# Feed-forward products by Strassen's algorithm over pairs of sequences, with features on the partitions

## The chip, the cores and the metric

The kernel runs on one NeuronCore of a Trainium2 chip. The metric is the device time of one execution in microseconds, the median of several runs. The engines are named as the profile names them: PE is TensorE (matrix products, with PEld its weight loads), DVE is VectorE, ACT is ScalarE, POOL is GpSimd, SP is SyncE, which here only issues DMAs.

## The reference

Four sequences of 512 tokens with 256 features pass through a gated scan and then through a feed-forward stack, each with a norm before and behind and a residual around it. All is float32.

```python
x = x + ln(attn(ln(x)))          # ln over the 256 features, no weights
x = x + ln(ffn(ln(x)))

def attn(x):                     # E = 256, HD = 128, E2 = 512
    q = silu(x @ Wq1 @ Wq2);  v = x @ Wv
    a = exp(log_sigmoid(sigmoid(x @ Wk1 @ Wk2)));  k = 1 - a
    h[t] = a[t] * h[t-1] + k[t] * v[t]           # scan over the tokens
    out = q * h
    return (out * rsqrt(mean(out**2) + 1e-6) * norm_w) @ Wo

def ffn(x):                      # 6 blocks, hidden 1024
    for i in range(6):
        x = gelu(x @ W1[i].T + B1[i]) @ W2[i].T + B2[i] + x
        if i < 5: x = ln(x) * LN_G[i] + LN_B[i]
    return x
```

## The kernel before

One sequence is one group of 512 tokens. The norms and the residuals have tokens on the partitions (four tiles of 128 tokens by 256 features); the projections, the gates, the scan and the hidden layer have features on the partitions, so that the scan runs along the free dimension. `transposed` (L122 to L126) turns a normalized group with eight TensorE transposes into two banks of PSUM and copies them out, one on DVE and one on ACT.

The first part is the attention. All loads are issued at the start: x, the constants and the first two blocks of feed-forward weights on SP's queue, the attention's weights on ACT's. The biases and norm weights of the feed-forward part are loaded with one copy for each partition. `won` (L156) is Wo scaled by norm_w. `scan_part` makes, for each of four feature tiles, the products psk, psv and psq, the sigmoids on ACT, and nkv, q and the scan h on DVE; POOL makes o = q h. `out_part` multiplies o by won with tokens on the partitions (psy) and sums the squares with one-column matmuls (pss). It runs one sequence behind the scan.

The second part is the feed-forward stack: six blocks, and in each the four sequences one after another. `hidden_part` (L306, L313) makes eight 128x512 tiles of the hidden layer, two matmuls each, and ACT's Gelu takes each out of PSUM with the bias. `output_part` (L324) uses the hidden tiles as the stationary operand: for each of four token tiles eight 128x256 matmuls into po, then DVE adds the residual (L331) and takes the norm's statistics (L99, L100). The norm's square root is on ACT (L105), with a table load before and behind it, as Gelu has another table. Two DVE instructions normalize and apply the norm's weights (L338, L341), and POOL adds the second bias to what will be the next residual (`with_bias`, L279). The transposes of the next sequence stand between hidden and output part of this one. `ffn_input` joins the parts: it adds the attention's normalized output to x and normalizes again.

Two sets of weights are held (w1 and w2 with two buffers); block i + 1 is loaded when block i begins. The framework's scheduler orders the instructions of each engine and sets the semaphores.

Of the kernel before, what the change touches and what calls it, by code (L numbers as in the profile page):

```python
# [9 lines left out]
F32 = mybir.dt.float32  # L10
AF = mybir.ActivationFunctionType
ALU = mybir.AluOpType
PSUM = bass.MemoryType.PSUM

P = 128
# [3 lines left out]

@with_exitstack  # L20
def kernel(
    ctx: ExitStack,
    tc: tile.TileContext,
    x: bass.AP,  # [B, S, E]
    wq1: bass.AP,  # [E, HD]
    wq2: bass.AP,  # [HD, E2]
    wk1: bass.AP,  # [E, HD]
    wk2: bass.AP,  # [HD, E2]
    wv: bass.AP,  # [E, E2]
    wo: bass.AP,  # [E2, E]  # L30
    norm_w: bass.AP,  # [128, E2/128], column c holds features c*128 ..
    w1t: bass.AP,  # [NB, E, HID]
    b1: bass.AP,  # [128, NB, HID/128], likewise
    w2t: bass.AP,  # [NB, HID, E]
    b2: bass.AP,  # [NB, E]
    ln_g: bass.AP,  # [NB-1, E]
    ln_b: bass.AP,  # [NB-1, E]
    out: bass.AP,  # [B, S, E]
):
    """x += LN(attn(LN(x))); x += LN(ffn(LN(x))), one sequence (512 tokens) as a group.  # L40

    Norms and residuals have tokens on the partitions; projections, the gates and the
    scan have features on the partitions, so that the scan runs along the free dimension.
    """
# [4 lines left out]
    NT = S // P  # token tiles of a group  # L49
# [3 lines left out]
    assert HD == P and S == 512  # L53
# [3 lines left out]
    ypool = ctx.enter_context(tc.tile_pool(name="ypool", bufs=B))  # L57
    small = ctx.enter_context(tc.tile_pool(name="small", bufs=4))
    xtp = ctx.enter_context(tc.tile_pool(name="xtp", bufs=3))
    wpool = ctx.enter_context(tc.tile_pool(name="wpool", bufs=2))  # L60
    ps_t = ctx.enter_context(tc.tile_pool(name="ps_t", bufs=2, space=PSUM))

# [7 lines left out]
    # x of each sequence, token c*128+p at [p, c]; it becomes x + LN(attn) in place.  # L70
    xs = []
    for b in range(B):
        xb = xpool.tile([P, NT, E], F32, tag="x", name=f"x_{b}")
        nc.sync.dma_start(out=xb, in_=x[b].rearrange("(c p) e -> p c e", p=P))
        xs.append(xb)

    b1_s = const.tile([P, NB, NH], F32)
    b2_s = const.tile([P, NB, E], F32)
    g_s = const.tile([P, NB - 1, E], F32)
    be_s = const.tile([P, NB - 1, E], F32)  # L80

    def load_ffn_constants():
        nc.sync.dma_start(out=b1_s, in_=b1)
        for t, src in ((b2_s, b2), (g_s, ln_g), (be_s, ln_b)):
            nc.sync.dma_start(out=t, in_=src.partition_broadcast(P))
# [9 lines left out]

    def token_stats(mv, src, t):
        """mean and variance over the free dim of src [128, E] into mv[:, t, :]"""
        st = small.tile([P, 6], F32, tag="bnst", name="st")
        nc.vector.bn_stats(st, src)  # L99
        nc.vector.bn_aggr(mv[:, t, :], st)  # L100

    def rstd_of(mv):
        """1 / sqrt(var + LN_EPS) of the tiles of a group"""
        std = small.tile([P, NT], F32, tag="std", name="std")
        nc.scalar.activation(std, mv[:, :, 1], AF.Sqrt, bias=eps_t)  # L105
        rstd = small.tile([P, NT], F32, tag="rstd", name="rstd")
        nc.vector.reciprocal(rstd, std)
        return rstd

    def normalized(dst, src, mv, scale, t):  # L110
        """dst = (src - mean) * scale of token tile t"""
        nc.vector.tensor_scalar(  # L112
            dst, src, mv[:, t, 0:1], scale[:, t : t + 1], ALU.subtract, ALU.mult
        )

    def transposed(src):
        """[128 tokens, NT, E] -> [128 features, ND, S]"""
        xt = xtp.tile([P, ND, S], F32, tag="xt", name="xt")
        for d in range(ND):
            pt = ps_t.tile([P, S], F32, tag="pt", name="pt")  # L120
            for t in range(NT):
                nc.tensor.transpose(pt[:, ts(t, P)], src[:, t, ts(d, P)], ident)  # L122
            if d % 2:
                nc.scalar.copy(xt[:, d, :], pt)
            else:
                nc.vector.tensor_copy(xt[:, d, :], pt)  # L126
        return xt

    ys, yscale_in, ymv = [None] * B, [None] * B, [None] * B

    with ExitStack() as actx:
# [3 lines left out]
        xnp = actx.enter_context(tc.tile_pool(name="xnp", bufs=B))  # L135
        ps_m = actx.enter_context(tc.tile_pool(name="ps_m", bufs=4, space=PSUM))
        ps_y = actx.enter_context(tc.tile_pool(name="ps_y", bufs=1, space=PSUM))

# [4 lines left out]
        wq2_s = aw.tile([P, E2], F32)  # L143
        nc.scalar.dma_start(out=wq2_s, in_=wq2)
# [3 lines left out]
        nc.scalar.dma_start(out=wv_s, in_=wv.rearrange("(c p) f -> p c f", p=P))  # L148
        wo_s = aw.tile([P, NE, E], F32)
        nc.scalar.dma_start(out=wo_s, in_=wo.rearrange("(c p) e -> p c e", p=P))  # L150
        nw_s = aw.tile([P, NE], F32)
        nc.scalar.dma_start(out=nw_s, in_=norm_w)
        # norm_w scales the rows of Wo: (out * norm_w) @ Wo
        won = aw.tile([P, NE, E], F32)
        for e in range(NE):
            nc.vector.tensor_scalar(  # L156
                won[:, e, :], wo_s[:, e, :], nw_s[:, e : e + 1], None, ALU.mult
            )

        load_ffn_constants()  # L160
        load_weights(0)
        load_weights(1)
        xns = []
        for b in range(B):
            mv = small.tile([P, NT, 2], F32, tag="mv", name="mv")
            for t in range(NT):
                token_stats(mv, xs[b][:, t, :], t)
            rstd = rstd_of(mv)
            xn = xnp.tile([P, NT, E], F32, tag="xn", name="xn")
            for t in range(NT):  # L170
                normalized(xn[:, t, :], xs[b][:, t, :], mv, rstd, t)
            xns.append(xn)

        def hidden(w1_s, xt, name):
            ps = ps_m.tile([P, S], F32, tag="m", name=f"ps_{name}")
            for d in range(ND):
                nc.tensor.matmul(  # L177
                    ps, w1_s[:, d, :], xt[:, d, :], start=(d == 0), stop=(d == ND - 1)
# [5 lines left out]
        def scan_part(b, xt):  # L184
            q1 = hidden(wq1_s, xt, "q1")
            k1 = hidden(wk1_s, xt, "k1")
            o = opool.tile([P, NE, S], F32, tag="o", name="o")
            sq = opool.tile([P, NE, S], F32, tag="sq", name="sq")
            for e in range(NE):
                psk = ps_m.tile([P, S], F32, tag="m", name="psk")  # L190
                nc.tensor.matmul(psk, wk2_s[:, ts(e, P)], k1, start=True, stop=True)  # L191
                psv = ps_m.tile([P, S], F32, tag="m", name="psv")
                for d in range(ND):
# [3 lines left out]
                        xt[:, d, :],  # L197
                        start=(d == 0),
                        stop=(d == ND - 1),
                    )  # L200
                psq = ps_m.tile([P, S], F32, tag="m", name="psq")
                nc.tensor.matmul(psq, wq2_s[:, ts(e, P)], q1, start=True, stop=True)  # L202

                # exp(log_sigmoid(f)) is sigmoid(f)
# [7 lines left out]
                # nkv = (a - 1) v;  h_t = a_t h_(t-1) - nkv_t  # L212
# [8 lines left out]
            return o, sq  # L221

        def out_part(b, o, sq):
            """y = (out * norm_w) @ Wo before the RMS scale r, with its mean and variance.

            LN(r y) = (y - mean) / sqrt(var + LN_EPS / r^2), 1/r^2 = mean(out^2) + RMS_EPS.
            """
            y = ypool.tile([P, NT, E], F32, tag="y", name=f"y_{b}")
            mv = ypool.tile([P, NT, 2], F32, tag="ymv", name=f"ymv_{b}")
            pss = ps_y.tile([P, NT], F32, tag="ss", name="pss")  # L230
            for t in range(NT):
                psy = ps_y.tile([P, E], F32, tag="y", name="psy")
# [177 lines left out]
```

## Time and profile before

| | us |
|---|---|
| runs | 860.53, 856.35, 859.64; median 859.64 |
| span of the profiled execution | 853.8 |
| PE busy | 815.0 (95%) |
| DVE, ACT, POOL busy | 310.7, 278.7, 109.4 |
| first feed-forward product in the chain of waits | 161.47 |
| 32 ph instructions of one sequence | 13.73 to 13.79 |
| 64 po instructions of one sequence | 13.81 |
| mean granted TensorE clock | 0.983 |

The span runs from the first to the last instruction of one execution; the page gives no other time of that execution, so the device time of the runs is set beside it. Busy time is the time in which an engine has an instruction running; for PE the end of a matmul is modelled. In a row of a group the two numbers behind the bar are the total busy time and the mean duration of one, and then comes the idle time of the engine before these instructions, with what ended it. One float32 matmul of the code appears as two MATMUL instructions in the trace.

### The profile page before, as it was taken

The numbers are of one execution on the slowest core, as the hardware profiler recorded it, in microseconds if no ns is written. First come the engines' busy times: TensorE is split into PE (matmuls) and PEld (weight loads), VectorE is DVE, ScalarE is ACT, GpSimd is POOL, SyncE is SP. The second block draws the span as 40 slices with busy tenths as digits, with TensorE's granted clock in tenths as the row PEclk, the third lists the DMA queues.
The fourth block names the chain that finished last, engine by engine and source line by source line (L and its number), as shares of the span: only waits on it lengthen the run. The fifth ranks groups of instructions, "written<-read, shape, count | busy, mean of one in ns | idle before, by whom it ended". The sixth has DMA issues, their size and how long they took to land.

```text
span 853.8 us, 7481 instructions
## 1 busy us (share of the span) xinstructions
PE 815.0 (95%) x2944; PEld 536.8 (63%) x2944; DVE 310.7 (36%) x750; ACT 278.7 (33%) x403; POOL 109.4 (13%) x134
## 2 busy tenths in 40 slices
PE   1999998699999999999999999999999999999996
PEld 0447657376577567765776577657765776577655
DVE  4562551725542334233423342334233423331223
ACT  1463451424421422242224222422243224322430
POOL 0120210201040111011101110111011101110111
PEclk9998999799999999999999999999999999999998
DMA  9400000000001100011000020000110000000000
GB/s 333 147 1 0 1 1 0 1 0 1 0 1 50 49 1 0 1 50 49 1 1 0 1 99 1 1 0 1 50 49 1 0 1 1 0 25 0 26 25 25
DMA packets 14674, 21.21 MB, mean 25 GB/s; under 512 B 944, under 2 KB 12208, under 8 KB 14640
## 3 DMA queue, kind: packets, MB, share of 16 engines
q1 hardware_dynamic: 12864, 18.90, 6.4%
q10 hardware_dynamic: 1776, 1.84, 0.6%
q8 instruction: 23, 0.38, 0.2%
q14 instruction: 11, 0.09, 0.0%
HBM read 18.64 MB, written 2.10 MB: 24 GB/s over the span
## 4 chain that ended last, share of the span: by engine, by line
PE 92%; issue 3%; DVE 2%; DMA 2%; POOL 0%; ACT 0%; POOLq 0%; ACTq 0%; DVEq 0%
PE ph L306 38%; PE po L324 37%; PE psy L234 4%; PE psv L194 3%; PE pt L122 3%; PE pss L242 2%; PE psk L191 2%; PE psq L202 2%; DMA nw_s<-in_norm_w 1%; PE ps_q L177 1%; PE ps_k L177 1%; DMA wk_s<-in_wk 1%; DVE xn L112 0%; DVE st L99 0%; DVE z L112 0%
## 5 line engine op out<-in xcount | busy, mean ns | idle before, releaser
L306 PE MATMUL ph<-xt,w 128*128 128x512 f32 x768 | 336.6, 596 | 0.9 <-DVE xt L126 0.9
L324 PE MATMUL po<-w,ht 128*128 128x256 f32 x1536 | 335.5, 379 | 0.0
L324 PEld LDWEIGHTS po<-w,ht 128*128 128x128 f32 x1536 | 290.0, 190 | 38.9 <-issue 0.5
L306 PEld LDWEIGHTS ph<-xt,w 128*128 128x128 f32 x768 | 146.4, 191 | 176.3 <-issue 170.7
L313 ACT ACTIVATE ht<-ph,b_s 128x512 f32<-128x512 f32 x192 | 129.4, 687 | 141.2 <-PE ph L306 140.9
L279 POOL TENSOR_TENSOR res<-f,b_s 128x256 f32<-128x256 f32 x96 | 76.7, 821 | 533.5 <-DVE f L341 438.3
L331 DVE TENSOR_TENSOR s<-po,res 128x256 f32<-128x256 f32 x96 | 40.8, 425 | 243.7 <-PE po L324 230.4
L105 ACT ACTIVATE std<-mv,eps_t 128x4 f32<-128x4 f32 x32 | 9.5, 297 | 282.2 <-DVE mv L100 282.0
L126 DVE COPY xt<-pt 128x512 f32<-128x512 f32 x28 | 19.3, 690 | 184.4 <-PE pt L122 184.4
L338 DVE SCALAR_TENSOR_TENSOR z<-s,mv,g_s 128x256 f32<-128x256 f32 x80 | 53.7, 691 | 1.4
L105 ACT ACT_TABLE_LOAD x29 | 37.2, 1283 | 51.9 <-DVE mv L100 44.0
L99 DVE BATCH_NORM_STATS2 st<-s 128x6 f32<-128x256 f32 x96 | 41.1, 428 | 3.3
L234 PE MATMUL psy<-won,o 128*128 128x256 f32 x128 | 35.5, 426 | 2.4 <-ACT y L249 2.4
L122 PEld LDWEIGHTS pt<-ident,f 128*128 128x128 f32 x192 | 22.9, 143 | 20.3 <-issue 18.8
L341 DVE SCALAR_TENSOR_TENSOR f<-z,rstd,be_s 128x256 f32<-128x256 f32 x80 | 35.5, 484 | 0.6
L234 PEld LDWEIGHTS psy<-won,o 128*128 128x128 f32 x128 | 26.7, 213 | 13.3 <-ACT y L249 5.5
L313 ACT ACT_TABLE_LOAD x27 | 34.6, 1283 | 0.5
L219 POOL TENSOR_TENSOR o<-q,h 128x512 f32<-128x512 f32 x16 | 20.3, 1268 | 107.8 <-DVE h L218 57.7
L122 PE MATMUL pt<-ident,f 128*128 128x128 f32 x192 | 26.6, 280 | 6.4 <-DVE f L112 6.4
L194 PE MATMUL psv<-xt,wv_s 128*128 128x512 f32 x64 | 30.1, 592 | 0.0
L347 POOL TENSOR_TENSOR s<-s,x 128x256 f32<-128x256 f32 x16 | 11.8, 764 | 99.8 <-issue 50.1
L122 PE MATMUL pt<-ident,xn 128*128 128x128 f32 x32 | 6.1, 334 | 18.8 <-DVE xn L112 18.1
(48 smaller groups left out, 323.8 us busy)
## 6 DMA issues: line engine op xcount, KB each, us to landing
w<-in_w1t SPq DMA_DIRECT2D x6, 1024.0 KB, 5.1
w<-in_w2t SPq DMA_DIRECT2D x6, 1024.0 KB, 5.6
x<-in_x SPq DMA_DIRECT2D x4, 512.0 KB, 7.6
out<-s SPq DMA_DIRECT2D x16, 128.0 KB, 1.7
b_s<-in_b SPq DMA_DIRECT2D x1, 768.0 KB, 7.7
g_s<-in_ln_g SPq DMA_DIRECT2D x1, 640.0 KB, 8.6
be_s<-in_ln_b SPq DMA_DIRECT2D x1, 640.0 KB, 8.1
wv_s<-in_wv ACTq DMA_DIRECT2D x1, 512.0 KB, 8.4
```

The source lines that it names most:

```text
L99: nc.vector.bn_stats(st, src)
L105: nc.scalar.activation(std, mv[:, :, 1], AF.Sqrt, bias=eps_t)
L122: nc.tensor.transpose(pt[:, ts(t, P)], src[:, t, ts(d, P)], ident)
L194: nc.tensor.matmul(psv, wv_s[:, d, ts(e, P)], xt[:, d, :], start=(d == 0), stop=(d == ND - 1),)
L234: nc.tensor.matmul(psy, o[:, e, ts(t, P)], won[:, e, :], start=(e == 0), stop=(e == NE - 1),)
L279: nc.gpsimd.tensor_tensor(r[:, t, :], f[:, t, :], b2_s[:, i, :], ALU.add)
L306: nc.tensor.matmul(ph, w1_s[:, d, ts(c, P)], xt[:, d, :], start=(d == 0), stop=(d == ND - 1),)
L313: nc.scalar.activation(ht[:, c, :], ph, AF.Gelu, bias=b1_s[:, i, c : c + 1])
L324: nc.tensor.matmul(po, ht[:, c, ts(t, P)], w2_s[:, c, :], start=(c == 0), stop=(c == NH - 1),)
L331: nc.vector.tensor_tensor(s[:, t, :], po, r[:, t, :], ALU.add)
L338: nc.vector.scalar_tensor_tensor(z, s[:, t, :], mv[:, t, 0:1], g_s[:, i, :], ALU.subtract, ALU.mult)
L341: nc.vector.scalar_tensor_tensor(f[:, t, :], z, rstd[:, t : t + 1], be_s[:, i, :], ALU.mult, ALU.add)
```

## The change

The feed-forward part is rewritten; the attention is reordered with it.

- Two sequences form one group. For each of the two weight products the weights, the features and the two sequences are seen as 2 by 2 blocks, and seven block products (Winograd's form of Strassen's algorithm) stand for eight. A hidden tile pair takes seven 128x512 matmuls instead of eight, the output part 28 instead of 32.
- The weights' block sums s1 to s4 are made on POOL, eight 128x512 additions for each block. The input's block sums t1 to t4 are made on DVE and POOL, for the normalized input (`tx`) and for each hidden tile pair (`tc`).
- Products p1, p6, p7 and p4 add up in one bank (px); after each ACT copies the running sum out (`sn`), or in the output part DVE adds it to the residual and the bias. The others are added to these copies by DVE before the Gelu.
- Both products have the weights as the stationary operand, so the output has features on the partitions. `norm_part` transposes it to tokens, takes the statistics, normalizes on DVE, and transposes back; the norm's weight and bias are applied when the second transposes are copied out. The constants are now one column for each feature tile.
- TensorE's order is written by hand (`manual_schedule`, `interleaved`): the norm of one pair of sequences stands in pieces between the products of the other pair, one piece after each fifth product.
- In the attention x of the first sequence is loaded in four pieces, some loads move from ACT's queue to SP's, k comes before q, won is made on POOL, POOL adds pairs of squares so that pss has half the matmuls, and out_part and the first `ffn_input` are interleaved with the scan of later sequences.

```diff
+    ctx.enter_context(tc.manual_schedule(engines={PE}))
...
+    def block_sums(a11, a12, a21, a22, shape, tag):
...
+        tt = nc.gpsimd.tensor_tensor
+        tt(s1, a21, a22, ALU.add)
+        tt(s3, a11, a21, ALU.subtract)
+        tt(s2, s1, a11, ALU.subtract)
+        tt(s4, a12, s2, ALU.subtract)
...
+    def to_features(src, d, tag, pool, scale=None, bias=None):
...
+        elif d % 2:
+            nc.scalar.activation(xt, pt, AF.Identity, scale=scale, bias=bias)
+        else:
+            nc.vector.tensor_scalar(xt, pt, scale, bias, ALU.mult, ALU.add)
...
+                if e % 2:
+                    nc.gpsimd.tensor_tensor(
+                        sq[:, e, :], sq[:, e, :], sq[:, e - 1, :], ALU.add
+                    )
...
+    def token_sums(b11, b12, b21, b22, pool, tag, engines):
...
+        engines[0].tensor_tensor(t1, b12, b11, ALU.subtract)
+        engines[2].tensor_tensor(t3, b22, b12, ALU.subtract)
+        engines[1].tensor_tensor(t2, b22, t1, ALU.subtract)
+        engines[3].tensor_tensor(t4, b21, t2, ALU.subtract)
...
+            def copied(self):
+                s = snp.tile([P, S], F32, tag="sn", name="sn")
+                nc.scalar.copy(s, self.px)
+                return s
...
+            def added(self, half, n, ps, s):
+                nc.vector.tensor_tensor(self.new(half, n), ps, s, ALU.add)
+                self.gelu(half, n)
...
+                engines = (POOL, DVE, POOL, DVE) if j < NP - 1 else (DVE, DVE, POOL, DVE)
+                tc4[j] = token_sums(*ht[j], *ht[NP + j], tcp, "tc", engines)
+
+        for j in range(0, NP, 2):
+            a, c = Pair(j), Pair(j + 1)
+            yield from a.p1()
+            yield from a.p2()
+            yield from c.p1()
+            yield from a.p6()
+            yield from c.p2()
+            yield from c.p6()
+            yield from a.p7()
+            yield from a.p5()
+            yield from c.p7()
+            yield from a.p4()
+            yield from c.p5()
+            yield from c.p4()
+            yield from a.p3()
+            yield from c.p3()
...
+        yield from product(px, a11, b11, True)
+        sn1 = partial(px, x11, 0)
+        yield from product(py, a12, b21, True)
+        nc.vector.tensor_tensor(sf[0][0], py, sn1, ALU.add)
+        yield from product(px, s2, t2, False)
+        sn2 = partial(px, x12, 0)
+        yield from product(pz, s1, t1, True)
+        yield from product(px, s3, t3, False)
+        sn3 = partial(px, x22, 1)
+        nc.vector.tensor_tensor(sf[1][1], pz, sn3, ALU.add)
+        yield from product(px, a22, t4, False)
+        with_bias(sf[1][0], px, x21, 1)
+        yield from product(pz, s4, b22, False)
+        nc.vector.tensor_tensor(sf[0][1], pz, sn2, ALU.add)
...
+    def norm_part(i, g):
...
+                    nc.tensor.transpose(
+                        pt[:, ts(2 * k + d, P)], sf[d][n][:, ts(t, P)], ident
+                    )
...
+            nc.scalar.copy(sm.rearrange("p a b -> p (a b)"), pt)
...
+        rstd = rstd_of(mv, nt)
...
+        for g in range(NG):
+            interleaved(chain_of(hidden_part(i, g), output_part(i, g)), pending, 6, 5)
+            pending = norm_part(i, g)
...
+        if i + 1 < NB:
+            sums1[i + 1] = w1_sums(i + 1)
+            sums2[i + 1] = w2_sums(i + 1)
```

## The prediction

> **What bounds the kernel now.** I read the page first (busy shares, the chain that ended last, the costliest groups), then the chain in order of time, then windows for the clock, then the timeline of single instructions.
>
> ```profile
> span 853.8 us, 7481 instructions
> PE 815.0 (95%) x2944; PEld 536.8 (63%) x2944; DVE 310.7 (36%) x750; ACT 278.7 (33%) x403; POOL 109.4 (13%) x134
> L306 PE MATMUL ph<-xt,w 128*128 128x512 f32 x768 | 336.6, 596 | 0.9 <-DVE xt L126 0.9
> L324 PE MATMUL po<-w,ht 128*128 128x256 f32 x1536 | 335.5, 379 | 0.0
> L313 ACT ACTIVATE ht<-ph,b_s 128x512 f32<-128x512 f32 x192 | 129.4, 687 | 141.2 <-PE ph L306 140.9
> ```
>
> TensorE never waits in the feed-forward part. The chain in order of time gives its pace:
>
> ```profile
> 147.11 2.01 PE psy L234 x8
> 149.56 2.01 PE psy L234 x8
> 157.16 2.19 DVE f L112 x4
> 161.47 9.67 PE ph L306 x16
> ...
> 249.76 13.79 PE ph L306 x32
> 264.42 13.81 PE po L324 x64
> 278.23 13.79 PE ph L306 x32
> ```
>
> A pass over one sequence is 32 ph instructions in 13.73 to 13.79 us, 0.87 us of eight transposes, 64 po in 13.81: 28.42 us. The chip runs each 128x512 product of the code as two instructions, so one product is 13.73 / 16 = 0.858 us. Two sequences take 56.8 us, the whole part 161.5 to 845.9, the tail to the end of the span 7.9.
>
> **TensorE's share of the change.** A pair of sequences is now 56 products (28 hidden, 28 output) instead of 64: 56 x 0.858 = 48.0 us. Features on the partitions cost transposes both ways, 32 instead of 16: 32 x 0.109 = 3.5. That is 51.5 us against 56.8, and 12 x 5.3 = 64 us would be the gain if TensorE still never waited.
>
> **Waits that the products now have.** In Strassen's form one bank, px, holds a running sum: a product is added, the bank is copied out, the next product is added. So TensorE waits for ACT's copies in the hidden part and for DVE's partial sums in the output part, and all engines work in the order of the built program. I laid one steady pair of sequences out by hand against that order with these rows: copy 0.59 (L124, 586), gelu 0.69 (L313), PSUM add 0.68 (q<-psq,sg, 677), SBUF two-input 512 columns on DVE 0.68 (x<-x,z, 417 for 256, most of it per column), the same on POOL 1.27 (o<-q,h, 1268), stats 0.43 and 0.18, matmul end to ACT's start 0.2.
>
> - First half of the hidden part (blocks 0 and 1): two products lie between a copy and its next use, 1.72 us, and 7 copies and gelus per 6 us of products fit on ACT. No wait.
> - Second half: in DVE's order the token sums of blocks 0 and 1 (t2, t4, t2, t4) and two stats stand before the add that makes this half's first gelu input, and in ACT's order that gelu stands before the copy that releases product c.p7. The chain from the end of the first half: gelu ready +0.8, POOL t1 1.27, POOL t3 1.27 and t1 1.27 of the next block, DVE t2 0.68, stats 0.43, t4 0.68, aggregate 0.18, stats 0.43, add 0.69, gelu 0.69, copy 0.59: 9.0 us. TensorE gets there after 8 products and 8 transposes, 7.7. Wait **1.3 us**, if DVE and POOL don't disturb each other.
> - Hidden to output: ACT's order puts the norm's square root with its two table loads before this half's last four gelus, DVE's order the reciprocal and eight normalizations before the last two adds, and the first partial sum of px behind the last token sums. From 0.7 before the hidden part's end: load 1.28, root 0.30, reciprocal 0.18, eight normalizations 2.67 (xn, x8), add 0.69, gelu 0.69, POOL t1 1.27, four DVE sums 2.72, partial 0.69, some 0.4 of hand-overs: ends 10.2 after the hidden part. The first two output products are 8 matmuls and 8 transposes, 7.7. Wait **2.5 us** before the third.
> - Third-last to second-last output product: both add into px with nothing between; drain 0.2, partial 0.69, 0.05: **0.95 us**.
>
> That is 4.75 us of waits at least. The upper end comes from this pair of rows: the same instruction alone, and beside a POOL addition.
>
> ```profile
> 244.10 0.48 DVE L338 SCALAR_TENSOR_TENSOR z<-s,mv,g_s 128x256 f32<-128x256 f32 x1
> ...
> 253.51 0.83 POOL L279 TENSOR_TENSOR res<-f,b_s 128x256 f32<-128x256 f32 x1 [11.47 <-DVE f L341]
> 253.68 0.95 DVE L338 SCALAR_TENSOR_TENSOR z<-s,mv,g_s 128x256 f32<-128x256 f32 x1
> ```
>
> z had 0.66 us of res ahead of it and took 0.47 longer. The token sums are of this kind: DVE's t2 needs POOL's t1, and POOL starts t3 at once, just as t2 becomes ready. If each waits the other's instruction out, the second half's chain gains 2.0 (wait 3.3), the hand-over to the output gains two POOL instructions less an overlap, 2.4 (wait 4.9), and the sums for the next hidden part, which DVE's order puts before the third partial sum, add 1.5 (wait 2.5): 10.7 us. A pair of sequences is then 56.3 to 62.2 us. I take 0.47 / 0.66 = 0.7 of the way, **60.4 us**, against 56.8 before.
>
> [...]
>
> **Before and around the feed-forward part.** First ph was at 161.5.
> - Start: DVE's won waits for norm_w until 16.30, and xn stands behind it at 17.58; won goes to POOL, norm_w and the broadcast constants (2 MB) out of the way. Stats on the first sequence stood at 6.95, but in DVE's new order two stats of the second, whose load was there at 7.33, precede the reciprocal: 8.2; root hidden, reciprocal 0.2, four normalizations 1.35, transposes and copies 2 to 3: first projection near 12 instead of 23.96. -12.
> - The 9.9 us from psy's end at 151.57 to ph: the first input's norm now lies beside the last scan. In its place the last out_part waits for the scan: f 0.60, a 0.63, nkv 0.69, q 0.68, h 1.28, o 1.27, less the three psy and four transposes before it, then the square 0.63 and POOL's new addition 1.27: 5. Net -5.
> - pss is halved: four bursts of 3.46 become 1.7 each, -7; the half clock that follows three of them (0.50 in the windows 68 to 74, 102 to 104, 136 to 138) cost 6, of which I expect 4 back.
> - POOL makes the first block's weight sums (8 x 1.27) before the first o: up to 3 later. +2.5.
> First product at 161.5 - 12 - 5 - 7 - 4 + 2.5 = 136.
> - First pair only: DVE does two sequences of ffn_input inside it, about 2 x 4 x (0.45 + 0.42 + 0.43 + 0.18 + 0.41) = 15 us, and ACT three pairs of table loads; roughly 9 not hidden (4 to 14).
> - Tail: 16 transposes with copies 3, last stats 1, load and root 1.6, norms, eight POOL additions at 0.76, output 2: 15 instead of 7.9.
> - Weight sums of later blocks: eight POOL additions, 10 us per two pairs; POOL has slack, their clash with DVE is in the upper end. Weight loads, 2 MB per block, lie under 100 us of work. Nothing.
>
> **Sum.** 136 + 12 x 60.4 + 9 + 15 = 885 against the profiled span of 853.8. The median of the runs, 859.64, stands 5.8 above that span; the page has no other time of the profiled execution. 885 + 5.8 = **891 us**. Without any DVE-POOL clash 136 + 675 + 24 + 5.8 = 841; with full exclusion 912. Equal times need a pair in (853.8 - 136 - 24) / 12 = 57.8 us, 6.3 us of waits.
>
> **Rivals.**
> 1. *Faster: the clash is small at 512 columns.* DVE's and POOL's instructions slip past each other, waits stay at 4.75 us: 841 us. It decides from under 6.3 us of waits per pair. For it: in the row 254.31 POOL's next res, 0.90, is hardly longer than 0.83. Against it: every z beside a res is near 0.95. 0.29.
> 2. *Much slower: the wait before the third output product drops the clock.* These windows (PE busy, PEld, DVE, ACT, POOL, then the granted clock) show 4.3 us of idle TensorE followed by 0.5:
>
> ```profile
> 152.00:154.00 2.00, 0.00 (x0) 0.00 (x0) 2.00 (x9) 1.27 (x1) 0.00 (x0) 1.00 0.01 4
> 154.00:156.00 2.00, 0.00 (x0) 0.00 (x0) 2.00 (x9) 0.00 (x0) 0.00 (x0) 1.00 0.00 0
> 156.00:158.00 2.00, 0.34 (x2) 0.30 (x2) 1.64 (x8) 0.39 (x2) 0.26 (x1) 0.59 0.00 0
> 158.00:160.00 2.00, 1.65 (x7) 0.96 (x7) 2.00 (x3) 0.00 (x0) 2.00 (x4) 0.50 0.00 0
> ```
>
> A wait of 4.9 is as long; some 3.4 us at half speed (about what the windows from 100.9 to 104.5 show) lose 1.7 in each of twelve pairs: 912 + 20 = 932. Against it: the gaps of 0.4 us at 138 to 152 left the clock at 1.0, and 0.7 of the way means 4.2 us. 0.13.
> 3. *The change doesn't give seven for eight in time.* Products that each wait for their own copy lose the overlap of weight load and drain, as psk<-k does at 49.74: 1.12 us for one product where the one in mid-stream at 41.75 shows 1.02, after 0.30 of waiting. A quarter of a microsecond on some 20 products of a pair is 5 us, 60 in all, on top of rival 1: 901. For it: most hidden products come after a copy or an add that releases their bank. Against it: psq and psk in mid-stream run at the full pace. 0.06.
>
> The forecast itself has 0.52, with 866 to 912 of its own. Under 840 lies perhaps 0.1 (rival 1 with a better start), over 930 as much (rival 2): range **840 to 930**. A difference within 0.5%, 4.3 us, is about what a measurement of this kernel can't tell from no change; rival 1 gives faster 0.25 and same 0.04, the forecast's lower edge 0.04 and 0.02, all else is slower: 0.29, 0.06, 0.65.
>
> **What would show it.** In the changed profile: PE busy near 740 us of a longer span; products at 0.43 per instruction; TensorE waiting three times per pair of sequences, for ACT's sn and DVE's partial sums, 6 to 10 us together; DVE sums of 512 columns above 0.9 us mean where POOL's run; first hidden product near 136 us. I am wrong if these waits are below 6 us per pair, if the sums show 0.7, or if the first product comes far from 136.

## The result and the profile after

The changed kernel takes **930.9 us** (median of four runs, 930.3 to 933.5) against 860.0 (856.4 to 860.5): 1.087 times the time before, 95% interval 1.082 to 1.093. Forecast were 891 us and a range of 840 to 930: the side is right, the size 40 us too low, and the range misses the time by 0.9 us. The profiled execution took 930.8 us, its span is 928.9.

The page after, in the same parts as before: span, busy times, the share of each engine in the chain that ended last, the granted clock in 40 slices, and the groups that matter (total and mean duration, then idle time before them and what ended it).

```profile
span 928.9 us, 6362 instructions
PE 783.4 (84%) x2112; PEld 371.1 (40%) x2112; DVE 522.3 (56%) x930; ACT 352.3 (38%) x565; POOL 251.7 (27%) x194
PEclk9998897999989999899999899998999998999998
PE 36%; DVE 28%; issue 17%; ACT 12%; POOL 5%; DMA 1%; POOLq 0%; DVEq 0%; ACTq 0%
L408 PE MATMUL px<-tc,sb 128*128 128x512 f32 x192 | 110.3, 717 | 41.2 <-DVE sn L530 38.7
L408 PE MATMUL px<-tx,sa 128*128 128x512 f32 x192 | 98.6, 606 | 32.6 <-ACT sn L437 32.6
L394 DVE TENSOR_TENSOR tc<-ht,tc 128x512 f32<-128x512 f32 x48 | 70.9, 1476 | 25.7 <-POOL tc L392 25.7
```

PE is busy 31.6 us less than before and the span is 75.1 longer: TensorE now waits. DVE carries 28% of the last chain. The third output product (px<-tc,sb) shows 717 ns an instruction where undisturbed products show 593: part of it ran at a lower clock (0.50 in the windows below). The row of tc has sums of 512 columns at 1.48 us, twice what the prediction's rows gave for one alone.

What TensorE waited for (us in total, times, longest), from the view of waits:

```profile
PE px L408 <- DVE sn L530: 62.5, 24, 4.2
PE px L408 <- ACT sn L437: 34.6, 15, 2.6
PE pt L163 <- DVE xn L154: 16.0, 3, 12.7
PE pt L163 <- DVE z L154: 7.4, 3, 3.5
```

The first two lines are the feed-forward part, 24 waits for DVE's partial sums and 15 for ACT's copies: nearly all of them stand in the three places that the prediction named. In TensorE's timeline of one steady pair of sequences (start, us, then in brackets the idle time before and its releaser) they are:

```profile
437.08 1.13 PE L408 MATMUL px<-tx,sa 128*128 128x512 f32 x2 [2.61 <-ACT sn L437]
454.01 5.12 PE L408 MATMUL px<-tc,sb 128*128 128x512 f32 x8 [3.53 <-DVE sn L530]
469.09 3.70 PE L408 MATMUL px<-tc,w 128*128 128x512 f32 x8 [2.21 <-DVE sn L530]
```

The eight instructions at 454.01 take 5.12 us, those at 469.09 3.70. The windows around 454 (PE busy, PEld, DVE, ACT, POOL, then the granted clock) say why: 3.5 us of idle TensorE, then half the clock.

```profile
450.00:452.00 2.00, 0.48 (x5) 0.24 (x3) 2.00 (x2) 0.78 (x1) 1.55 (x1) 1.00 0.00 0
452.00:454.00 2.00, 0.00 (x0) 0.00 (x0) 2.00 (x5) 0.00 (x0) 0.00 (x0) 0.88 0.00 0
454.00:456.00 2.00, 1.99 (x3) 0.96 (x4) 1.16 (x2) 0.00 (x0) 0.00 (x0) 0.50 0.00 0
456.00:458.00 2.00, 2.00 (x5) 0.88 (x4) 0.00 (x0) 0.00 (x0) 0.00 (x0) 0.77 0.00 0
```

What DVE did in the meantime, from its timeline:

```profile
443.03 0.20 DVE L149 RECIPROCAL rstd<-std 128x8 f32<-128x8 f32 x1 [2.07 <-ACT std L147]
443.27 2.67 DVE L154 TENSOR_SCALAR n<-sm,mv,rstd 128x256 f32<-128x256 f32 x8
445.86 1.28 DVE L453 TENSOR_TENSOR ht<-pz,sn 128x512 f32<-128x512 f32 x2
...
448.68 1.74 DVE L394 TENSOR_TENSOR tc<-ht,tc 128x512 f32<-128x512 f32 x1 [0.82 <-POOL tc L392]
450.35 1.75 DVE L392 TENSOR_TENSOR tc<-ht 128x512 f32<-128x512 f32 x1
452.02 0.68 DVE L395 TENSOR_TENSOR tc<-ht,tc 128x512 f32<-128x512 f32 x1
```

and POOL, from its own:

```profile
447.37 1.27 POOL L392 TENSOR_TENSOR tc<-ht 128x512 f32<-128x512 f32 x1 [14.10 <-ACT ht L443]
448.60 2.95 POOL L393 TENSOR_TENSOR tc<-ht 128x512 f32<-128x512 f32 x2
```

Two things are seen. The eight normalizations of the other pair of sequences stand in DVE's queue, with 2.07 us of waiting for the square root, ahead of the last two adds of the hidden part (445.86), on which all that follows depends. And a DVE sum that starts just after a POOL sum takes 1.74 or 1.75 us; as soon as POOL is done (451.55) the next takes 0.68. The alternation is a strict one: POOL's two take 2.95 instead of 2 x 1.27.

The first feed-forward product stands at 160.31, hardly earlier than before (161.47).

### The profile page after: what moved, and what is told of

Read it like the earlier page. It is cut to its first block, busy times and chain, and to the rows that moved or that the text cites. A ratio compares the mean times of both kernels' runs of the same rounds, so it can differ in the third digit from the quotient of the medians.

```text
span 928.9 us, 6362 instructions
## 1 busy us (share of the span) xinstructions
PE 783.4 (84%) x2112; PEld 371.1 (40%) x2112; DVE 522.3 (56%) x930; ACT 352.3 (38%) x565; POOL 251.7 (27%) x194
## 3 DMA queue, kind: packets, MB, share of 16 engines
q10 hardware_dynamic: 1104, 1.31, 0.4%
## 4 chain that ended last, share of the span: by engine, by line
PE 36%; DVE 28%; issue 17%; ACT 12%; POOL 5%; DMA 1%; POOLq 0%; DVEq 0%; ACTq 0%
PE px L408 16%; PE pz L408 8%; DVE tc L394 7%; ACT ht L443 5%; DVE n L154 4%; DVE tc L395 3%; POOL tc L392 3%; PE psy L336 3%; DVE ht L453 2%; DVE tc L392 2%; DVE st L141 2%; PE pt L163 2%; ACT L147 2%; PE psv L278 2%; ACT sn L437 1%
## 5 line engine op out<-in xcount | busy, mean ns | idle before, releaser
L443 ACT ACTIVATE ht<-ht,b_s 128x512 f32<-128x512 f32 x144 | 102.6, 721 | 124.9 <-DVE ht L453 77.1
L408 PE MATMUL px<-tc,sb 128*128 128x512 f32 x192 | 110.3, 717 | 41.2 <-DVE sn L530 38.7
L437 ACT COPY sn<-px 128x512 f32<-128x512 f32 x144 | 81.0, 581 | 146.8 <-PE px L408 146.8
L392 POOL TENSOR_TENSOR tc<-ht 128x512 f32<-128x512 f32 x36 | 51.4, 1426 | 314.3 <-ACT ht L443 314.3
L408 PE MATMUL px<-tx,sa 128*128 128x512 f32 x192 | 98.6, 606 | 32.6 <-ACT sn L437 32.6
L394 DVE TENSOR_TENSOR tc<-ht,tc 128x512 f32<-128x512 f32 x48 | 70.9, 1476 | 25.7 <-POOL tc L392 25.7
L453 DVE TENSOR_TENSOR ht<-pz,sn 128x512 f32<-128x512 f32 x96 | 64.6, 684 | 30.3 <-ACT ht L443 17.0
L393 POOL TENSOR_TENSOR tc<-ht 128x512 f32<-128x512 f32 x48 | 71.0, 1490 | 0.0
L530 DVE SCALAR_TENSOR_TENSOR sn<-px,b_s,xt 128x512 f32<-128x512 f32 x36 | 26.7, 742 | 62.0 <-PE px L408 62.0
L408 PE MATMUL px<-tx,w 128*128 128x512 f32 x96 | 52.0, 624 | 2.0 <-ACT sn L437 2.0
L408 PE MATMUL pz<-tx,sa 128*128 128x512 f32 x96 | 49.9, 602 | 0.0
L408 PE MATMUL px<-xt,w 128*128 128x512 f32 x96 | 49.1, 593 | 0.0
```

The lines of the kernel that those rows point to most:

```text
L392: engines[0].tensor_tensor(t1, b12, b11, ALU.subtract)
L393: engines[2].tensor_tensor(t3, b22, b12, ALU.subtract)
L394: engines[1].tensor_tensor(t2, b22, t1, ALU.subtract)
L408: nc.tensor.matmul(ps, l, r, start=start and k == 0, stop=True, skip_group_check=True)
L437: nc.scalar.copy(s, self.px)
L443: nc.scalar.activation(h, h if src is None else src, AF.Gelu, bias=b1_s[:, i, c : c + 1])
```

## The experiments

Theories: **A**, POOL's and DVE's sums exclude each other, and that makes TensorE wait. **B**, the norm's place in DVE's queue, ahead of the last adds and the sums, makes it wait. **C**, the idle time costs a second time, by the clock. For the first product: TensorE's hand-written order in the attention waits for norms. A time in the table is that of one execution, for the changed kernel, e5_all, e6_old_ffn and e7_split the median of four; the kernel before took 852.0 to 859.8 beside them. Where an edit moves work on the other engines, the scheduler orders their queues anew.

| run | edit to the changed kernel | us | PE waits for sn (DVE, ACT) |
|---|---|---|---|
| changed kernel | | 930.9 | 62.5, 34.6 |
| e1_tc_dve | hidden sums all on DVE | 888.7 | 24.3, 11.0 |
| e2_warm | three dummy products before the long wait | 909.4 | 36.1, 33.9 |
| e3_norm_later | norm pieces later | 869.3 | 17.2, 35.8 |
| e4_attn | order of the norms in the attention | 906.1 | 56.4, 34.5 |
| e9_both | e1 and e3 | 820.7 | 10.1, 4.3 |
| e11_no_table | no square root, so no table loads | 950.5 | 70.3, 34.0 |
| e5_all | e1, e3, e4, input sums on DVE, output order | 787.3 | 0, 6.7 |
| e7_split | e5 with the sums shared again | 837.5 | 7.0, 35.8 |
| e8_pool_all | e5 with the hidden sums all on POOL | 810.1 | 0, 6.7 (and 15.3 for tc) |
| e6_old_ffn | e4 with the feed-forward part of before | 825.8 | |

### A alone: the sums of the hidden block on DVE (e1_tc_dve)

```diff
-                engines = (POOL, DVE, POOL, DVE) if j < NP - 1 else (DVE, DVE, POOL, DVE)
+                engines = (DVE, DVE, DVE, DVE)
```

> All four token sums of each hidden tile pair (tc) on DVE; POOL keeps only the weight sums, tx t3 and the attention's work. Theory A (DVE and POOL shut each other out for whole instructions): the sums t2 of 1.48 us mean fall to 0.68, the chain between the halves of the hidden part shortens by about 2 us although DVE now has seven more instructions per pair, and the wait before c.p7 (2.6 us) falls under 1; the wait before the third output product stays near 3.5, since DVE now does eight sums one after another there. About 2 to 3 us per pair of sequences: 895 to 905 us. Theory B (only the place in the queues counts, not the other engine): the sums stay as long in the way, 920 to 935 us.

888.7 us, 42 less. DVE has more instructions and is faster through them. Its groups and TensorE's waits:

```profile
L392 DVE TENSOR_TENSOR tc<-ht 128x512 f32<-128x512 f32 x48 | 35.9, 748 | 0.9 <-ACT ht L443 0.2
L394 DVE TENSOR_TENSOR tc<-ht,tc 128x512 f32<-128x512 f32 x48 | 32.8, 682 | 0.0
```

```profile
PE pz L408 <- DVE ht L453: 24.8, 11, 3.1
PE px L408 <- DVE sn L530: 24.3, 12, 2.3
```

L394 falls from 1476 to 682 ns. The wait before the third output product is gone, where I had expected it to stay near 3.5. A new one takes part of its place (pz for ht, 24.8, 1.30 and 3.07 us in turn): it ends with an add of the hidden part that stands behind six normalizations of the other pair in DVE's queue (in one pair they run from 482.25 to 486.04, the add from 485.96). That is B's place in the queue, still there. A holds, and the gain is larger than I expected of it. It isn't the length of the sums alone: DVE's waiting for POOL's sums (25.7 us in the row of tc of the changed kernel) goes with it.

### C alone: the same wait, with TensorE kept busy (e2_warm)

```diff
         nc.vector.tensor_tensor(sf[0][0], py, sn1, ALU.add)
+        pw = ps_m.tile([P, S], F32, tag="m", name="pw")
+        for k in range(3):
+            nc.tensor.matmul(pw, a12[k], b21[k], start=True, stop=True)
```

> Three extra products into an unused PSUM bank behind the second output product, where TensorE waits 3.5 us; nothing reads them. If the half clock after that wait comes from the idle TensorE, it goes and with it 1.5 us in each of eleven pairs, though TensorE does 31 us more work: 910 to 916 us. If the clock follows something else, or the extra products push the third one back: 930 to 935 us.

909.4 us. The dummy products, which nobody reads, fill 2.6 us of the wait; what is left of it is 0.96 to 1.63, together as long as before, and the product behind takes 3.70 instead of 5.1 to 6.8. The other two waits of a pair stay at 2.55 and 2.21. Ten steady pairs take 614.7 us here and 634.4 in the changed kernel: the half clock costs 2.0 us a pair, some 20 of the 21.5 us. Most of the rest lies ahead of the feed-forward part, which starts about 1.2 us earlier.

### B alone: the norm's pieces later (e3_norm_later)

The first piece of the norm comes after the fourth product instead of the sixth, the next ones after every eighth instead of every fifth. The square root then lies behind the last gelu, and the normalizations behind the sums.

```diff
-            interleaved(chain_of(hidden_part(i, g), output_part(i, g)), pending, 6, 5)
+            interleaved(chain_of(hidden_part(i, g), output_part(i, g)), pending, 4, 8)
```

> The pieces of the other pair's norm stand behind every eighth product from the fourth on, not every fifth from the sixth; in the built order the square root with its table loads then comes behind this half's last gelu and the eight normalizations behind the token sums. Theory B (place in the queues): the wait before the third output product falls from 3.5 us plus 1.5 us of half clock to under 1, that before c.p7 from 2.6 to about 1 as adds now stand before two of the token sums, that before the second-last output product to about 1: 5 to 6 us in each of eleven pairs, 865 to 875 us. Theory A alone (the exclusion of DVE and POOL, wherever they stand): the sums keep their 1.48 us and less than 15 us is won, 915 or more.

869.3 us, 62 less, with the exclusion untouched (L394 at 1480 ns). DVE's timeline at the same point of a pair:

```profile
422.06 0.69 DVE L453 TENSOR_TENSOR ht<-pz,sn 128x512 f32<-128x512 f32 x1 [0.17 <-PE pz L408]
...
424.03 1.74 DVE L394 TENSOR_TENSOR tc<-ht,tc 128x512 f32<-128x512 f32 x1 [0.45 <-POOL tc L392]
...
430.25 2.67 DVE L154 TENSOR_SCALAR n<-sm,mv,rstd 128x256 f32<-128x256 f32 x8
```

The last add runs as its product ends, the sums follow, and the 2.67 us of normalizations lie behind them. The waits for DVE's sn go from 62.5 to 17.2 and no longer drop the clock (the longest is 0.97, and the product behind it takes 3.70). B is the largest single factor. The waits for ACT's sn come to 35.8 as before (34.6), but they are 38 now instead of 15: in place of the 2.6 before one product of the second half of the hidden part a pair has 0.40, 0.63 and 1.73 before three.

### Do A and B cure the same wait? (e9_both)

Both edits, nothing else.

> The changed kernel with two edits that were each tried alone: the hidden block's sums all on DVE (alone: 888.7 us, 42 less than the changed kernel) and the norms behind these sums (alone: 869.3 us, 62 less). If they cure different waits their gains add: 931 - 42 - 62 = 827 us. If they cure the same wait twice over, only the larger one counts: 855 to 869 us. The attention and the order of the output products are untouched, so it should lie above the run with all edits (787) by what those two bring, 25 us for the attention and the rest for the order.

820.7 us: 110 less, where the single gains add to 104. By the expectation the edits then cure different waits, but the waits don't say so. Each edit alone takes away most of the wait before the third output product and the half clock behind it (3.53 to 4.20 us of waiting become 0 in e1 and at most 0.97 in e3). What each leaves behind alone makes up for that: e1 leaves the 24.8 us for ht, behind the norm that e3 moves, and 2.27 before the second-last product, mostly with half clock behind it (the product takes 5.40 us instead of 3.70); e3 leaves the 35.8 for ACT's sn. With both edits the first is gone, the second is 0.84 and the third 4.3. That the gains add is thus a sum that happens to come out. With these two edits the kernel is already some 35 us faster than before (856.1 beside it).

### Is it ACT's table loads? (e11_no_table)

```diff
-        nc.scalar.activation(std, mv[:, :, 1], AF.Sqrt, bias=eps_t)
+        nc.scalar.activation(std, mv[:, :, 1], AF.Sqrt if nt == NT else AF.Identity, bias=eps_t)
```

> The changed kernel, but the square root of the norms behind the output products is left out (ACT copies the variance plus epsilon in its place), so the two table loads of 1.28 us around it go and its place in ACT's queue stays. If the eight normalising instructions ahead of the last hidden sums in DVE's queue are what makes TensorE wait, they still stand there and start 1.3 us earlier: the waits before the third output product fall by 1.3 to 2.6 us of a pair and the half clock behind them partly goes, 931 - 12 x 1.3..3.5 = 889 to 915 us. If ACT's table loads are the whole cause, the result is that of the run with the norms behind the sums: 865 to 875 us. If neither, 925 to 931 us.

950.5 us, 20 more: outside all three. The normalizations do come earlier, as the first case had it: they start 4.76 us behind the product of c.p7 (446.40 and 441.64), in the changed kernel 6.19 (443.27 and 437.08). But the scheduler, which ordered the other engines anew, now puts an application of the norm's weights (L173) and the last sum (L395) ahead of the partial sum (L530) that TensorE waits for, and these two take 1.32 us of the 1.43 back. In the timelines of DVE and TensorE and in the windows:

```profile
456.35 0.80 DVE L173 TENSOR_SCALAR xt<-pt,g_s,be_s 128x512 f32<-128x512 f32 x1
457.07 0.67 DVE L395 TENSOR_TENSOR tc<-ht,tc 128x512 f32<-128x512 f32 x1
457.67 0.74 DVE L530 SCALAR_TENSOR_TENSOR sn<-px,b_s,xt 128x512 f32<-128x512 f32 x1
```

```profile
458.46 6.77 PE L408 MATMUL px<-tc,sb 128*128 128x512 f32 x8 [3.43 <-DVE sn L530]
```

```profile
456.00:458.00 2.00, 0.00 (x0) 0.00 (x0) 2.00 (x4) 0.00 (x0) 0.00 (x0) 0.96 0.00 0
458.00:460.00 2.00, 1.53 (x2) 0.84 (x3) 1.10 (x2) 0.00 (x0) 0.00 (x0) 0.50 0.00 0
...
462.00:464.00 2.00, 2.00 (x4) 0.93 (x3) 0.00 (x0) 0.00 (x0) 0.00 (x0) 0.50 0.00 0
464.00:466.00 2.00, 2.00 (x5) 0.72 (x5) 0.72 (x1) 0.00 (x0) 0.00 (x0) 0.83 0.00 0
```

The wait is as long as in the changed kernel (3.43 and 3.53 us), but the half clock lasts longer: 0.96 in the first and 0.83 in the last of these windows, with 0.50 between, put it from about 457.8 to 464.7, 6.8 us, where in the changed kernel 0.88 and 0.77 put it from 453.5 to 456.9, 3.4. The product takes 6.77 instead of 5.12. In the other pairs the wait is 4.87 (4.20 in the changed kernel). So this run doesn't clear the table loads: without them the chain to DVE's sums was 1.4 us shorter, and the order of DVE's queue was worth as much. What the loads alone cost in time stays open, and so does how long the half clock lasts, which the length of the wait doesn't tell.

### The first product: the norms in the attention (e4_attn)

All four input norms are made at the start. The first feed-forward norm is begun ahead of the third out_part, and its transposes come one piece later in TensorE's order.

```diff
-        for _ in attn_input(0):
+        ins = [attn_input(b) for b in range(B)]
+        for it in ins:
+            next(it)
+        for _ in ins[0]:
...
             if b + 1 < B:
-                side.append(attn_input(b + 1))
+                side.append(ins[b + 1])
+            if b == 3:
+                first = ffn_input(0)
+                next(first)
+                side.append(iter([None]))
             if b:
                 side.append(out_part(b - 1))
             if b == 3:
-                side.append(ffn_input(0))
+                side.append(first)
```

> The feed-forward part as in the change. In the attention the norms of all four inputs are made at the start, as in the kernel before, and the first feed-forward input's norm is put ahead of the third out_part instead of behind it. If the late attention comes from TensorE waiting in its fixed order for these norms (xn, z: 11 us of waits behind the start, each followed by some us of half clock), the first feed-forward product comes near 145 instead of 160 us and the time is near 916 us. If it is the scan's own chain over ACT, DVE and POOL that sets the pace, it stays above 155.

906.1 us, 25 less, and the first product stands at 139.31 instead of 160.31. These lines of the changed kernel's timeline are what went:

```profile
70.64 1.03 PE L163 MATMUL pt<-ident,xn 128*128 128x128 f32 x3 [2.34 <-DVE xn L154]
...
127.48 0.88 PE L163 MATMUL pt<-ident,z 128*128 128x128 f32 x3 [2.87 <-DVE z L154]
...
138.71 1.35 PE L163 MATMUL pt<-ident,z 128*128 128x128 f32 x4 [3.52 <-DVE z L154]
```

TensorE takes its queue in the written order: a transpose whose norm isn't ready holds up the products behind it. The waits for z and the later ones for xn are 10.6 us. The clock was 0.91 on the mean from 15 to 160 us, and is 0.96 here from 15 to the first product: 0.09 x 145 = 13 us lost against 0.04 x 125 = 5. Together 18.6 of the 21.

### Everything together, and what each part is worth there (e5_all, e7_split, e8_pool_all)

e5_all has the edits of e1, e3 and e4, and two more: the input sums `tx` on DVE, and a bank of its own for the product that stood behind the third-last, so that it covers the drain.

```diff
-        txs[g] = token_sums(b11, b12, b21, b22, txp, "tx", (DVE, DVE, POOL, DVE))
+        txs[g] = token_sums(b11, b12, b21, b22, txp, "tx", (DVE, DVE, DVE, DVE))
...
         nc.vector.tensor_tensor(sf[1][1], pz, sn3, ALU.add)
+        nc.vector.tensor_tensor(sf[0][1], pz, sn2, ALU.add)
+        pw = ps_m.tile([P, S], F32, tag="m", name="pw")
+        yield from product(pw, s4, b22, True)
+        nc.vector.tensor_tensor(sf[0][1], pw, sf[0][1], ALU.add)
         yield from product(px, a22, t4, False)
         with_bias(sf[1][0], px, x21, 1)
-        yield from product(pz, s4, b22, False)
-        nc.vector.tensor_tensor(sf[0][1], pz, sn2, ALU.add)
```

> All five edits at once: the four sums of the hidden block and of the input block all on DVE, the side work stepped so that the square root comes behind the last gelu, the attention of the earlier experiment (input norms at the start, the first feed-forward norm ahead of the third output projection), and the product before the third-last output product taken into a bank of its own. Theory A (DVE is slowed beside POOL) and theory B (the norms stand ahead of the sums in DVE's queue) together: the three waits of a pair fall to 0 to 2.5 us in sum, so a pair is 51.5 to 54 us and the whole 139.8 + 12 x 51.5..54 + 14 + 2 = 774 to 804 us. Rival: with all sums on DVE its work per pair (some 36 us of 52) is spread so that the next product waits for it; pairs stay above 56 us and the whole above 828.

**787.3 us** (787.1 to 787.5), 0.919 of the kernel before, 95% interval 0.916 to 0.923. Its page and TensorE's largest waits:

```profile
span 785.1 us, 6319 instructions
PE 742.1 (95%) x2112; PEld 359.4 (46%) x2112; DVE 502.8 (64%) x1038; ACT 349.1 (44%) x563; POOL 107.7 (14%) x98
```

```profile
PE pt L163 <- DVE xn L154: 13.0, 1, 13.0
PE px L416 <- ACT sn L445: 6.7, 15, 1.2
```

This lies within the 774 to 804 of A and B together. DVE does nearly all that POOL did, and the rival I gave, that TensorE comes to wait for DVE's work, is out: the same product of successive pairs starts at 410.04, 462.67 and 515.22, 52.6 us apart, 1.1 above the 51.5 of TensorE's own work.

e7_split gives the sums back to both engines.

```diff
-                engines = (DVE, DVE, DVE, DVE)
+                engines = (POOL, DVE, POOL, DVE) if j < NP - 1 else (DVE, DVE, POOL, DVE)
...
-        txs[g] = token_sums(b11, b12, b21, b22, txp, "tx", (DVE, DVE, DVE, DVE))
+        txs[g] = token_sums(b11, b12, b21, b22, txp, "tx", (DVE, DVE, POOL, DVE))
```

> The run with all edits, but the sums of the hidden and the input block again shared between POOL and DVE. If the exclusion costs only where the order of DVE's queue is bad, this is within 10 us of the run with all edits (its waits are covered). If it costs on its own, the sums of 1.48 us in place of 0.7 leave the first hidden-to-output wait of a pair at 1.0 to 1.5 us, and the whole is 12 x 1 to 2 = 12 to 24 us longer than the run with all edits.

837.5 us, 0.978 of the kernel before, 95% interval 0.974 to 0.983: 50 more than e5_all, twice the upper end of what I expected. The good order doesn't cover the exclusion (the row of L402 is at 1480 ns, in e5_all at 684); the waits for ACT's sn are back at 35.8.

e8_pool_all puts the four hidden sums of e5_all on POOL.

```diff
-                engines = (DVE, DVE, DVE, DVE)
+                engines = (POOL, POOL, POOL, POOL)
```

> The run with all edits, but all four sums of every hidden block on POOL alone. A sum alone on POOL took 1.27 us and one alone on DVE 0.68 to 0.75. If only the use of both engines on one chain of sums is harmful, DVE's other sums (0.68) stay at 0.7 and the chain of four takes 5.1 us in place of 2.8: the last wait before an output product grows by 2.3 us, 787 + 12 x 0 to 2.5 = 787 to 817 us. If POOL's sums slow whatever of two inputs in SBUF runs on DVE, and are slowed by it, the cost is like that of the split, 835 us or more, and DVE's sums that read PSUM show whether they are touched: 0.68 or above 0.9.

810.1 us. One engine alone, even the slower one (1.29 us a sum on POOL, 0.68 on DVE in e5_all), is 27 us better than the two in turns (e7_split shares the input sums too). What is left against e5_all lies in every second pair: the others take 52.55 us (255.70 to 308.25), as in e5_all. In the slower pairs four weight sums stand in POOL's queue ahead of the last hidden sums (438.65 to 443.80 in one pair), and TensorE waits 2.94 to 3.22 us for tc, the 15.3 us of the table, in some pairs with slower products behind it (eight instructions at 454.37 take 4.68 us instead of 3.60). Its groups show which DVE instructions POOL's sums hold up:

```profile
L154 DVE TENSOR_SCALAR n<-sm,mv,rstd 128x256 f32<-128x256 f32 x96 | 95.0, 1050 | 0.4
L461 DVE TENSOR_TENSOR ht<-pz,sn 128x512 f32<-128x512 f32 x96 | 65.5, 683 | 78.1 <-ACT ht L451 41.4 <-PE pz L416 34.0 <-ACT sn L445 1.2
L402 POOL TENSOR_TENSOR tc<-ht,tc 128x512 f32<-128x512 f32 x48 | 62.0, 1292 | 0.0
```

The normalizations, one SBUF input and a SBUF output, go from 460 ns (e5_all) to 1050. The adds with one input in PSUM keep their 0.68. In one pair POOL's sums run without a break from 428.71 to 438.7, and DVE's timeline has in that stretch:

```profile
429.13 0.69 DVE L461 TENSOR_TENSOR ht<-py,sn 128x512 f32<-128x512 f32 x1 [0.60 <-ACT sn L445]
434.66 0.69 DVE L461 TENSOR_TENSOR ht<-pz,sn 128x512 f32<-128x512 f32 x1
```

The sums of the changed kernel, with two inputs in SBUF, held up both engines (1.74 and 1.75 us on DVE, 2.95 for two on POOL); the adds that read PSUM (0.68) are not held up here. Of the normalizations, with their one SBUF input, only DVE's side shows it: seven of them take 8.32 us from 444.57 on, about one for each of POOL's sums, but those sums take 1.31 us, hardly more than the 1.27 alone. Why POOL's sums are slowed by DVE's sums and hardly by its normalizations no run here shows.

### The feed-forward change by itself (e6_old_ffn)

The attention of e4_attn, then the feed-forward functions of the kernel before on their own token layout, in that kernel's order.

```diff
-        for g in range(NG):
-            interleaved(chain_of(hidden_part(i, g), output_part(i, g)), pending, 6, 5)
-            pending = norm_part(i, g)
...
+        for b in range(B):
+            r = with_bias(fs[b], i)
+            if i == 0 and b + 1 < B:
+                fs[b + 1] = ffn_norm(b + 1)
+            ht = hidden_part(i, xt)
...
+            fs[b] = output_part(i, b, ht, r)
```

> The feed-forward part of the kernel before (one sequence at a time, eight block products, norms on the token layout) behind the changed attention with its improved order. First hidden product near 140 us; the feed-forward of before took 684 us behind its first hidden product, so 140 + 684 + 8 of tail + 2 around = 834 us. It tells what the feed-forward change alone does: the run with the improved attention and the changed feed-forward took 906, so the changed feed-forward as it stands would cost 72 us. If the attention's order alters the feed-forward (constants late, first norm of the others late), up to 850.

825.8 us, 0.965 of the kernel before, 95% interval 0.961 to 0.968, with PE busy 97% of the span. So the two halves of the change part: with a good attention, the feed-forward part as it was changed costs 80 us (906.1 - 825.8), and in the order of e5_all it saves 38.5. Some 5 us of this lie ahead of the feed-forward part: the first hidden product stands at 134.54 here, at 139.31 in e4_attn and at 139.38 in e5_all (here one sequence's norm is made ahead of it, there two; that this is the reason wasn't tried). The feed-forward parts by themselves are thus some 75 us apart in the first case and 43 in the second.

## Why the prediction was right and wrong

**Right: the arithmetic of TensorE.** 51.5 us a pair is what e5_all reaches within 1.1, and PE is busy 742.1 us there where I had near 740. Rival 3 wanted 5 us a pair from products behind a wait; they show 1.12 or 1.13 us there instead of 1.02, so it is out at that price.

**Right: the three waits and their cause.** In the pair shown they are 2.61, 3.53 and 2.21 us, sum 8.35, between the ends 4.75 and 10.7 and 0.6 of the way where I took 0.7; with the 4.20 of every second pair it is 9.0. For the single sum the rows show the full exclusion (1.74 = the rest of POOL's sum and 0.56); the chains laid out by hand were a little long. Rival 1, a small clash, is out by these waits and by e1_tc_dve, which is 42 us faster without it.

**Wrong: the term of 60.4 us a pair, by the clock.** Steady pairs take 62.4 and 64.0 in turn, 63.1 on the mean of the eleven behind the first. The failed step is the clock behind the wait before the third output product, which the sum of 60.4 put at nothing. I held the half clock for rival 2's case alone, because the windows I had showed it after 4.3 us of idle, and reasoned that 0.7 of the way, 4.2 us, kept the wait below. I had misread these windows, too: by the timeline TensorE stood idle for 6.10 us there, from 151.55 to 157.66, and the clock fell some 4.8 us into it (the 0.59 of the third window puts that at 156.4). In the changed kernel it falls with waits of 3.53, and even with one of 2.18. With the 2.0 us a pair of e2_warm the forecast's pair is 62.4, and the eleven are 20 us longer. That was rival 2's price (932) without its condition, full exclusion in the sum of waits.

**Wrong: the term of 136 us for the first product.** Measured 160.3. The start brought 9 (first projection at 15.01 instead of 23.96) where I had 12. The 5 + 7 + 4 that I expected behind it did not come: from the first projection to the first product there are 145.3 us, before 137.5, and the clock, of which 4 us were to come back, is 0.91 there against 0.93. The failed step here is "the first input's norm now lies beside the last scan". Its DVE work does; its transposes stand in TensorE's fixed order ahead of the last sequence's later scan products and output projections and wait for it, as do xn's, and behind the three waits shown under e4_attn (2.34, 2.87 and 3.52 us) the clock falls to 0.50. I had walked TensorE's order by hand in the feed-forward part only. e4_attn, which moves these norms, brings 21.0 of the 24.3 us back.

**Too high:** nine for the first pair (it took 60.3 us, no more than forecast for any other), 15 for the tail (14.2) and 5.8 from span to time (2.0).

The sum, in spans: 885 + 24.3 (first product) + 29.7 (eleven pairs, 2.7 each) - 9.1 (first pair) - 0.8 (tail) = 929. Of the 29.7, about 20 are the clock. The rest may be TensorE's own work: an estimate with e5_all's 1.1 us above 51.5, the mean of the waits and e2_warm's 2.0 gives 51.5 + 1.1 + 8.7 + 2.0 = 63.3 for the 63.1, but no run shows the 1.1 in the changed kernel itself. The 4.20 in place of 3.53 in every second pair is the other engine again: there the eight normalizations begin at 379.27, while POOL makes a weight sum (378.94 to 380.21), and take 3.35 us instead of 2.67.

The chances followed the cases: the forecast's mechanism happened, rival 2's price came with it, and 0.65 for slower was if anything too little. Either of the two errors alone would have left the time inside the range (891 + 24, or 891 + 20); both on the side of more time, they carry it past the end at 930.

## What to carry to other kernels

A bank that holds a running sum ties TensorE to the engine that copies it out (62.5 and 34.6 us of waits here), so the place of every other instruction in that engine's queue becomes part of TensorE's time; before trading arithmetic for such ties, lay out the queue of the copying engine, and put work for later (norms of another group) behind it. Two engines don't always share work: here the sums given to one engine beat the split between DVE and POOL by 27 to 50 us. That the gains of two edits add doesn't show that they cure different waits; look at the waits that each leaves. Price a wait of TensorE at its length and the risk of a lost clock (2.0 us a pair here), and walk an order written by hand from the first instruction, not only where the change is meant to act.

## What the runs showed of the hardware

The half clock follows waits shorter than the row of before had led me to think, and not by length alone. The first two of these lines are the same product in two pairs of e1_tc_dve, the last is the third output product of one pair in the changed kernel:

```profile
448.94 5.40 PE L408 MATMUL px<-tc,w 128*128 128x512 f32 x8 [2.26 <-DVE sn L530]
688.69 3.70 PE L408 MATMUL px<-tc,w 128*128 128x512 f32 x8 [2.27 <-DVE sn L530]
```

```profile
327.12 5.40 PE L408 MATMUL px<-tc,sb 128*128 128x512 f32 x8 [2.18 <-DVE sn L530]
```

After some 2.27 us of idle the clock was once halved (0.50 from 450 to 452, the product takes 5.40 us) and once not (3.70 us). In the changed kernel 2.18 us before the third output product halved it (0.50 from 328 to 330), but 2.21 before the second-last product never cost anything (3.70 us each time). So gaps of 2.2 to 2.3 us already halved the clock at times; what decides beside their length no run here shows.
